# Layer 1 of a graph attention kernel: long tiles get their softmax in two or three groups of rows with all sums in PSUM

## The chip, the cores and the metric

The kernel runs on one core of a Trainium2 chip. The metric is the device time of one execution in microseconds; the time of the kernel before is 5602.67 us, the median of three runs (5597.33 to 5605.57). All arithmetic of the layers is in float32.

## The reference

A network of two graph attention layers on 10,000 nodes with 768 features, and 170,000 edges (80,000 random pairs in both directions and a loop at each node). The edges come sorted by their target `dst`. Every node gets a mean over the rows of its sources, weighted by a softmax over its own incoming edges; in layer 1 this is done for 4 heads of 256 columns, in layer 2 for one head of 768. `gat_conv` adds one more loop to each node.

```python
def gat_conv(x, edge_index, W, a_src, a_dst, bias, heads, out_ch, concat):
    ei = _add_self_loops(edge_index, n)
    src, dst = (ei[0], ei[1])
    xl = (x @ W).reshape(n, heads, out_ch)
    alpha_src = jnp.einsum('nhc,hc->nh', xl, a_src)
    alpha_dst = jnp.einsum('nhc,hc->nh', xl, a_dst)
    e = jax.nn.leaky_relu(alpha_src[src] + alpha_dst[dst], 0.2)
    m = jax.ops.segment_max(e, dst, num_segments=n)
    e = jnp.exp(e - m[dst])
    s = jax.ops.segment_sum(e, dst, num_segments=n)
    alpha = e / (s[dst] + 1e-16)
    msg = xl[src] * alpha[:, :, None]
    out = jax.ops.segment_sum(msg, dst, num_segments=n)
    ...

h0 = x
h = relu(layer_norm(gat_conv(x, ..., HEADS, HID, True), g1, be1))
h1 = h + (h0 @ Wr1 + br1)
h = layer_norm(gat_conv(h1, ..., 1, OUT_DIM, False), g2, be2) + (h1 @ Wr2 + br2)
result = layernorm(x + h)
```

## The kernel before

**Stages.** `prepare` sorts the nodes by their number of edges, while TensorE computes `table1`: a row for each node with 1024 columns of `x @ W1` and, behind them, 4 target terms, 4 source terms and a number, 1033 float32 in all. `ordered_layer1` then gathers and reduces these rows and writes `table2`, and `ordered_layer2` does the same for layer 2. A third path, `general_path`, is for inputs that don't fit and isn't run here.

**Tiles and slots.** A tile is 128 nodes, one on each partition. Since the nodes are sorted, all nodes of a tile have about as many edges; `SLOTS[t]` is the number of rows that tile t gathers for each of its nodes. A row or slot is therefore one gather of 128 rows of `table1`, at most 529 KB; empty places of a tile aren't loaded. There are 79 tiles and 1377 slots. `TURNS` puts the tiles in an order that grows from 8 slots (position 0) to 41 (position 39) and falls again to 9 (position 78). Positions 34 to 45 have 22, 22, 23, 24, 26, 41, 27, 25, 24, 23, 22, 22 slots; 33 and 46 have 21.

**The ring.** `Ring` holds `RING1` = 29 slots in SBUF. `ring.fetch(q + 1 + ring.size)` (L872) is called after row q has been added, and asks for the row that takes its place: a gather (L425) on POOL's queue, which waits there until the engines are done with the old row.

**One tile that fits into the ring** (`whole`, L779; 29 slots and less). `weights_of(t)` (L741) makes its softmax. `logits` (L473) adds the target's term to the source terms of all n rows (L479; two instructions where the ring wraps), applies the leaky slope (L189), takes the maximum over the rows (L483), subtracts it (L486), and lets ACT take the exponents (L487); then it turns the rows' numbers into slots for layer 2 (L490) and clears the last columns of the rows (L491). `normalised` (L494) doubles the loop's weight (L504), sums (L498), adds 1e-16 (L499), inverts (L500) and multiplies (L501). All of these are on DVE with 4 to 108 numbers a partition.

The rows are then added to `acc`, 128 x 1024 in PSUM, in three ways:

- the first 4 (`ON_PE1`) by PE: ACT writes 4 diagonal matrices a row with the weights (L730), and PE multiplies them with the row (L736);
- of the others, three in four (`shared`, L753) are multiplied in place by ACT (L510, four instructions a row) and added by DVE with one TENSOR_TENSOR (L517);
- one in four is weighted and added by DVE alone (L521, four SCALAR_TENSOR_TENSOR of 256 columns).

ACT multiplies `LEAD` = 3 rows ahead of DVE (L867).

**How tiles overlap.** The softmax of tile t+1 is begun inside the loop of tile t: its `logits` at row n-3, its `normalised` and the first two rows of PE's sums at row n-2 (L868), the other two at the head of the next turn (L796). This is done if `SLOTS[t + 1] + LEAD <= ring.size` (L864), which holds for all but positions 39 and 40. After the loop, the next turn takes the statistics of `acc` (L579, L581), normalises it (L593, L595), adds the product of x with `Wr1` (L807), transposes the outcome h on PE, multiplies it with `w2` (L829) and stores `table2`.

**The tile of 41 slots** doesn't fit into the ring. It isn't begun ahead, and goes through `attend_parts` (L524): three groups of rows with a running maximum. For each group there are `logits` with the old maximum (L485); 4 rows summed by PE into a PSUM tile of its own (`sums`), the others by DVE into `h`, 128 x 1024 in SBUF, which is cleared first (L531); ahead of each later group `sums` is added to `h` (L539) and `h` is multiplied by the exponent of old minus new maximum (`fade`, L541, L542, L545). At the end the sums are added and `divided` divides by the total (L436). Two thirds of the rows are multiplied by ACT, each just ahead of its addition.

**Queues and order.** Each engine executes its instructions in the order in which the code records them (`manual_schedule`); an instruction that waits holds back all behind it on its engine. Gathers of rows and of x stand in POOL's queue, the loads and stores of x, h and `table2` in SP's.

Of the kernel before, what the change touches and what calls it, by code (L numbers as in the profile page):

```python
# [28 lines left out]
F32 = mybir.dt.float32  # L29
# [6 lines left out]
P = 128  # L36
# [17 lines left out]
PARTED2 = 26  # L54

# [25 lines left out]
def gnn_kernel(ctx, tc, x, x_cols, src, dst, src_col, dst_col, W1, a_src1, a_dst1, b1, g1, be1, Wr1, br1,  # L81
# [421 lines left out]
    def doubled(e, t):  # L503
        nc.vector.tensor_scalar(e[:, 0], e[:, 0], loops[:, TURNS[t]:TURNS[t] + 1], None, op0=OP.mult)  # L504
# [7 lines left out]
    def weigh(acc, row, e, dh, first=None, shared=False):  # L512


        if shared:
            c = e.shape[1] * dh
            nc.vector.tensor_add(acc[:, :c], acc[:, :c], row[:, :c])  # L517
            return
        for h in range(e.shape[1]):
            s = slice(h * dh, (h + 1) * dh)  # L520
            nc.vector.scalar_tensor_tensor(acc[:, s], row[:, s], e[:, h:h + 1],  # L521
                                           (acc if first is None else first)[:, s], op0=OP.mult, op1=OP.add)

    def attend_parts(small, ring, acc, h_, ad, heads, dh, t, summed, between):  # L524


        c = heads * dh
        groups = -(-SLOTS[t] * 2 // ring.size)
        cuts = [FIRST[t] + SLOTS[t] * g // groups for g in range(groups + 1)]
        top = total = sums = None  # L530
        nc.vector.memset(acc[:, :c], 0.0)  # L531
        for lo, hi in zip(cuts, cuts[1:]):
            e, new = logits(small, ring, lo, hi, ad, heads, c, top)
            if lo == FIRST[t]:
                doubled(e, t)
            part = small.tile([P, heads], F32, name="part")
            nc.vector.reduce_sum(part, e.rearrange("p k h -> p h k"), axis=AX.X)
            if top is not None:
                nc.vector.tensor_add(acc[:, :c], acc[:, :c], sums[:, :c])  # L539
                fade = small.tile([P, heads], F32, name="fade")  # L540
                nc.vector.tensor_sub(fade, top, new)  # L541
                nc.scalar.activation(fade, fade, AF.Exp)  # L542
                for h in range(heads):
                    s = slice(h * dh, (h + 1) * dh)
                    nc.vector.tensor_scalar(acc[:, s], acc[:, s], fade[:, h:h + 1], None, op0=OP.mult)  # L545
                nc.vector.tensor_mul(fade, total, fade)
                nc.vector.tensor_add(part, part, fade)
            top, total = new, part
            m = min(ON_PE1, hi - lo - 1)
            pe = lo if hi == cuts[-1] else hi - m  # L550
            steps = summed(pe, e[:, pe - lo:], m)
            sums = next(steps)
            if pe == lo:
                for _ in steps:
                    pass
            alone = [q for q in range(lo, hi) if not pe <= q < pe + m]
            for k, q in enumerate(alone):
                shared = k >= len(alone) // 3
                if shared:
                    multiply(ring.slot(q), e[:, q - lo], dh)  # L560
                if k == len(alone) // 3 + 1:
                    for _ in steps:
                        pass
                weigh(acc, ring.slot(q), e[:, q - lo], dh, shared=shared)
                ring.fetch(q + 1 + ring.size)
            ring.fetch(hi + ring.size)
            between.pop(0)()
        nc.vector.tensor_add(acc[:, :c], acc[:, :c], sums[:, :c])
        divided(small, h_, acc, total, None, heads, dh)
# [116 lines left out]
    def ordered_layer1():  # L686
        nc.scalar.add_instruction(mybir.InstLoadActFuncSet(name=nc.get_next_instruction_name(), act_func_set_id=6, engine=nc.scalar.engine))
        with tc.tile_pool(name="b1", bufs=1) as pool, tc.tile_pool(name="small1", bufs=2) as small, \
# [32 lines left out]
            def on_pe(t):  # L721


                return min(max(SLOTS[t] // 2 - 5, 1), ON_PE1, SLOTS[t])
# [16 lines left out]
            def weights_of(t):  # L741

                n, m = SLOTS[t], on_pe(t)
                e, _ = logits(small, ring, FIRST[t], FIRST[t] + n, ring.slot(FIRST[t])[:, C1:C1 + H1], H1, C1)
                yield e
                normalised(small, e, H1, t)
                acc = ps_acc.tile([P, 2 * BANK], F32, name="acc")
                diagonals = pool.tile([P, ON_PE1 * H1, P], F32, name="diagonals")
                for lo, hi in ((0, min(m, 2)), (min(m, 2), m)):
                    summed(acc, diagonals, e, FIRST[t], lo, hi, m)  # L750
                    yield acc

# [22 lines left out]
            for t in range(NT + 1):  # L775
# [3 lines left out]
                whole = live and n <= ring.size  # L779
                if whole and not ready:  # L780
                    ahead = weights_of(t)
                    ready += itertools.islice(ahead, 2)

                def multiplied(upto):
                    nonlocal done
                    while whole and done < min(upto, n):
                        if shared(t, done):
                            multiply(ring.slot(FIRST[t] + done), e[:, done], DH1)
                        done += 1

                if whole:
                    e, acc = ready
# [3 lines left out]
                for _ in ahead:  # L796
                    pass
# [21 lines left out]
                if whole:  # L819
                    by_wr1()  # L820
# [26 lines left out]
                if live and not whole:  # L847
                    due(first + 1)
                    sums, acc = (ps_acc.tile([P, 2 * BANK], F32, name="acc") for _ in range(2))
                    ad = small.tile([P, H1], F32, name="ad")  # L850
                    nc.vector.tensor_copy(ad, ring.slot(FIRST[t])[:, C1:C1 + H1])

                    def some(q, e, m):
                        diagonals = pool.tile([P, ON_PE1 * H1, P], F32, name="diagonals")
                        for lo, hi in ((0, min(m, 2)), (min(m, 2), m)):
                            summed(sums, diagonals, e, q, lo, hi, m)
                            yield sums

                    h = pool.tile([P, C1], F32, name="h")
                    attend_parts(small, ring, h, acc, ad, H1, DH1, t, some,  # L860
                                 [by_wr1, lambda: due(n)] + [lambda: None] * n)
                ready = []
                ahead = iter(())
                if whole and t + 1 < NT and SLOTS[t + 1] + LEAD <= ring.size:  # L864
                    ahead = weights_of(t + 1)
                for k in range(n if whole else 0):
                    multiplied(k + 1 + LEAD)  # L867
                    if n - LEAD <= k < n - LEAD + 2:  # L868
                        ready += itertools.islice(ahead, 1)
                    if k >= first:  # L870
                        weigh(acc, ring.slot(FIRST[t] + k), e[:, k], DH1, shared=shared(t, k))
                    ring.fetch(FIRST[t] + k + 1 + ring.size)  # L872
                    due(k)
# [468 lines left out]
```

## Time and profile before

| | |
|---|---|
| runs, median (lowest, highest) | 5602.67 us (5597.33, 5605.57) |
| profiled execution | 5607.1 us, its span 5605.3 us |
| granted TensorE clock, mean | 0.93 |
| busy in the span: PE, DVE, ACT, POOL | 4888.6, 4294.8, 2813.9, 3242.1 us |
| layer 1, first to last write of h (L595) | 939.3 to 3410.7 us |

The span is what the profiler recorded from the first to the last instruction, and the time of the execution is a little longer. In the lists of waits a line names the waiting instruction, what released it, the microseconds in total, how often, and the longest.

DVE writes h once a tile (L595). The time from one of these writes to the next is the length of a tile; most of the softmax of the tile that follows lies in it too.

| position | slots | length, us | | position | slots | length, us |
|---|---|---|---|---|---|---|
| 20 | 17 | 29.5 | | 38 | 26 | 41.4 |
| 27 | 19 | 31.7 | | 39 | 41 | 81.0 |
| 30 | 20 | 33.5 | | 40 | 27 | 52.0 |
| 33 | 21 | 36.6 | | 41 | 25 | 43.9 |
| 34 | 22 | 39.3 | | 42 | 24 | 41.7 |
| 35 | 22 | 41.7 | | 43 | 23 | 41.5 |
| 36 | 23 | 43.1 | | 44 | 22 | 40.0 |
| 37 | 24 | 46.0 | | 45 | 22 | 39.1 |

### The profile page before, as it was taken

Reading aid. Unit: us, or ns where it says so; the run is one execution under the profiler, and the core shown is the slowest. Engines: PE = TensorE matmul, PEld = TensorE weight load, DVE = VectorE, ACT = ScalarE, POOL = GpSimd, SP = SyncE. Lnnn points to the kernel's source line nnn. Section 1 sums busy time; section 2 is a strip of 40 time slices with the busy share of each in tenths; the row PEclk is TensorE's granted clock in tenths of the full one; section 3 lists DMA queues with packets and bytes.
Section 4 is the critical chain, followed back from the end, with each engine's and each line's share of the span. In section 5 each row is a group of like instructions: output and inputs, shape, how many; then the busy total and the mean of one; then the engine's idle time right before and its main releaser. Section 6 shows DMA issues by size and latency. Waiting matters only on the chain. (4 is left out here: it accounts for less than half of the span.)

```text
span 5605.3 us, 59627 instructions
## 1 busy us (share of the span) xinstructions
PE 4888.6 (87%) x15188; PEld 2899.2 (52%) x15191; DVE 4294.8 (77%) x7761; ACT 2813.9 (50%) x8193; POOL 3242.1 (58%) x3159
## 2 busy tenths in 40 slices
PE   8999996999999875789999999899988888877765
PEld 3444443555555543455555555565655555555544
DVE  5783344999999887888999995888876866766676
ACT  3443344777788776777877773333322322222222
POOL 3447365556666556566666553666665666666664
PEclk9999998999999987899999999999998888888877
DMA  4333626999999987899999986999888888888885
GB/s 156 122 99 87 92 90 254 323 335 352 362 361 373 340 320 265 316 343 360 364 359 355 335 307 231 323 336 331 320 321 292 313 299 299 288 293 286 289 286 182
DMA packets 474307, 1591.37 MB, mean 284 GB/s; under 512 B 118328, under 2 KB 122488, under 8 KB 473959
## 3 DMA queue, kind: packets, MB, share of 16 engines
q0 software_dynamic: 322384, 1286.62, 64.8%
q1 hardware_dynamic: 149520, 297.43, 15.8%
q10 hardware_dynamic: 2054, 3.42, 0.2%
q8 instruction: 128, 2.10, 0.2%
q14 instruction: 221, 1.80, 0.1%
HBM read 1431.80 MB, written 177.29 MB: 287 GB/s over the span
## 5 line engine op out<-in xcount | busy, mean ns | idle before, releaser
L425 POOL DMA_INDIRECT ring<-table,slots x2675 | 2660.2, 994 | 1774.4 <-issue 542.1
L521 DVE SCALAR_TENSOR_TENSOR acc<-ring,e,acc 128x512 f32<-128x512 f32 (+1 forms) x2530 | 1578.3, 624 | 137.7 <-PE acc L736 46.1
L510 ACT ACTIVATE ring<-ring,e 128x256 f32<-128x256 f32 x3284 | 1338.3, 508 | 1.4 <-issue 1.2
L517 DVE TENSOR_TENSOR acc<-acc,ring 128x1024 f32<-128x1024 f32 x801 | 985.7, 1231 | 73.2 <-issue 1.9
L991 PE MATMUL big<-wr,w 128*128 128x512 f32 (+1 forms) x2464 | 876.7, 502 | 147.0 <-issue 145.5
L946 PE MATMUL big<-ring,diagonals 128*128 128x256 f32 x2754 | 746.9, 430 | 169.1 <-issue 138.7
L172 PE MATMUL big<-w,xT 128*128 128x512 f32 x1896 | 823.8, 596 | 26.5 <-DMA w<-in_W_dram 10.3
L172 PE MATMUL big<-wr,xT 128*128 128x512 f32 x1896 | 833.2, 596 | 0.2 <-issue 0.2
L829 PE MATMUL half<-w,hT 128*128 128x512 f32 (+1 forms) x2528 | 830.4, 486 | 0.0
L946 PEld LDWEIGHTS big<-ring,diagonals 128*128 128x128 f32 x2754 | 590.5, 218 | 331.3 <-issue 203.6
L991 PEld LDWEIGHTS big<-wr,w 128*128 128x128 f32 x2464 | 484.2, 197 | 504.0 <-issue 471.6
L945 ACT ACTIVATE diagonals<-ident,e 128x128 f32<-128x128 f32 x1377 | 423.9, 388 | 612.9 <-remote 230.0
L829 PEld LDWEIGHTS half<-w,hT 128*128 128x128 f32 x2528 | 477.8, 189 | 372.3 <-issue 332.7
L736 PE MATMUL acc<-ring,diagonals 128*128 128x256 f32 x1912 | 480.1, 408 | 204.8 <-ACT diagonals L730 179.6
L172 PEld LDWEIGHTS big<-w,xT 128*128 128x128 f32 x1896 | 361.3, 191 | 484.5 <-issue 466.3
L172 PEld LDWEIGHTS big<-wr,xT 128*128 128x128 f32 x1896 | 356.7, 192 | 420.3 <-issue 420.3
L736 PEld LDWEIGHTS acc<-ring,diagonals 128*128 128x128 f32 x1912 | 387.0, 205 | 290.7 <-ACT diagonals L730 200.8
L583 ACT ACTIVATE sd<-mv,eps 128x1 f32<-128x1 f32 x237 | 69.3, 292 | 697.5 <-DVE mv L581 451.6
L730 ACT ACTIVATE diagonals<-ident,e 128x128 f32<-128x128 f32 x956 | 293.0, 387 | 207.6 <-DVE e L501 165.4
L667 DVE TENSOR_TENSOR scr<-big,ad_b 128x1024 f32<-128x1024 f32 x79 | 96.7, 1224 | 377.5 <-ACT row L664 333.4
L672 POOL TENSOR_TENSOR row<-row,none 128x1024 f32<-128x1024 f32 x79 | 187.2, 2370 | 260.8 <-ACT row L664 258.4
L670 ACT ACTIVATE scr<-scr 128x256 f32<-128x256 f32 x632 | 253.6, 402 | 120.3 <-DVE scr L667 117.7
(185 smaller groups left out, 3430.6 us busy)
## 6 DMA issues: line engine op xcount, KB each, us to landing
ring<-table,slots POOLq DMA_INDIRECT x2675
table<-row SPq DMA_DIRECT2D x79, 516.0 KB
h_d<-hT SPq DMA_DIRECT2D x79, 512.0 KB
w<-h_d SPq DMA_DIRECT2D x77, 512.0 KB
table<-row SPq DMA_DIRECT2D x79, 385.0 KB
ring<-table SPq DMA_DIRECT2D x79, 385.0 KB
xT<-in_x_cols_dram SPq DMA_DIRECT2D x79, 384.0 KB
x_d<-xt SPq DMA_DIRECT2D x79, 384.0 KB
```

The lines of the kernel that those rows point to most:

```text
L172: nc.tensor.matmul(p[:, c:e], aT[:, j, :], w[:, j, c:e], start=(j == 0), stop=(j == k - 1))
L425: nc.gpsimd.indirect_dma_start(out=to, out_offset=None, in_=table, in_offset=bass.IndirectOffsetOnAxis(ap=index, axis=0), **more)
L510: nc.scalar.activation(row[:, s], row[:, s], AF.Copy, scale=e[:, h:h + 1])
L517: nc.vector.tensor_add(acc[:, :c], acc[:, :c], row[:, :c])
L521: nc.vector.scalar_tensor_tensor(acc[:, s], row[:, s], e[:, h:h + 1], (acc if first is None else first)[:, s], op0=OP.mult, op1=OP.add)
L670: nc.scalar.activation(m[:, s], m[:, s], AF.Copy, accum_out=row[:, C1 + i * H1 + h:C1 + i * H1 + h + 1])
L730: nc.scalar.activation(diagonals[:, k * H1 + i, :], ident, AF.Copy, scale=e[:, k, i:i + 1])
L736: nc.tensor.matmul(acc[:, c:d], diagonals[:, k * H1 + i, :], ring.slot(q + k)[:, c:d], start=(k == 0 and c % BANK == 0), stop=(k == m - 1 ...
L829: nc.tensor.matmul(q, hT[:, j, :], w2[:, j, c:c + q.shape[1]], start=(j == 0), stop=(j == K1 - 1))
L945: nc.scalar.activation(diagonals[:, (k - lo) % G, :], ident, AF.Copy, scale=e[:, k - lo, :])
L946: nc.tensor.matmul(to, diagonals[:, (k - lo) % G, :], ring.slot(at + k)[:, ON_PE2:C2], start=False, stop=(k == n - 1), skip_group_check=True)
L991: nc.tensor.matmul(r[:, c:d], hT[:, j, :], wr2[:, j, c:d], start=False, stop=(j == K1 - 1 and d < C2), skip_group_check=True)
```

## The change

Every tile now goes through the same loop, and `attend_parts` is gone. `cuts_of(t)` divides the rows of a tile: one group below `PARTED` = 22 slots, two from 22 to 29, three for 41. A cut that would fall on a row that DVE weights alone moves on by one, so that the first row of a later group is always one that ACT multiplies. The cuts are at 11 (22 and 23 slots), 13 (24 to 27 slots), and 13 and 27 (41 slots).

`weights_of(t)` makes the softmax of the first group alone, not yet divided by its sum, and begins PE's sums; this happens at the same places of the tile ahead as before, for every tile. The target's term is copied to `ad` first. For each later group it goes on inside the tile's own loop: eight rows ahead of the cut `logits` of the group with the old maximum, and the exponent `fade` of old minus new maximum; five rows ahead of the cut the new total, and in the last group the division of `fade` and of the group's weights by it. At the cut, `weigh` with `fade` multiplies all that is in `acc` and adds the row, in four SCALAR_TENSOR_TENSOR of 256 columns in place of one TENSOR_TENSOR. `acc` stays in PSUM throughout, also for the tile of 41 slots, of which only the first 4 rows are now summed by PE, and of the others three in four are multiplied by ACT. The condition on the ring's size at L864 is dropped.

Of the removed function only the ends are shown.

```diff
--- before.py
+++ after.py
@@ -52,6 +52,7 @@
 SHARE = 4
 ON_PE1 = 4
 PARTED2 = 26
+PARTED = 22
 
 
 def chunk_counts(n_edges):
@@ -509,9 +510,15 @@
             s = slice(h * dh, (h + 1) * dh)
             nc.scalar.activation(row[:, s], row[:, s], AF.Copy, scale=e[:, h:h + 1])
 
-    def weigh(acc, row, e, dh, first=None, shared=False):
-
-
+    def weigh(acc, row, e, dh, first=None, shared=False, fade=None):
+
+
+        if fade is not None:
+            for h in range(e.shape[1]):
+                s = slice(h * dh, (h + 1) * dh)
+                nc.vector.scalar_tensor_tensor(acc[:, s], acc[:, s], fade[:, h:h + 1], row[:, s],
+                                               op0=OP.mult, op1=OP.add)
+            return
         if shared:
             c = e.shape[1] * dh
             nc.vector.tensor_add(acc[:, :c], acc[:, :c], row[:, :c])
@@ -520,53 +527,6 @@
             s = slice(h * dh, (h + 1) * dh)
             nc.vector.scalar_tensor_tensor(acc[:, s], row[:, s], e[:, h:h + 1],
                                            (acc if first is None else first)[:, s], op0=OP.mult, op1=OP.add)
-
-    def attend_parts(small, ring, acc, h_, ad, heads, dh, t, summed, between):
...
-        divided(small, h_, acc, total, None, heads, dh)
 
     def pieces(a, width):
 
@@ -740,15 +700,50 @@
 
             def weights_of(t):
 
-                n, m = SLOTS[t], on_pe(t)
-                e, _ = logits(small, ring, FIRST[t], FIRST[t] + n, ring.slot(FIRST[t])[:, C1:C1 + H1], H1, C1)
-                yield e
-                normalised(small, e, H1, t)
+                n, m, at = SLOTS[t], on_pe(t), FIRST[t]
+                cuts = cuts_of(t)
+                ad = ring.slot(at)[:, C1:C1 + H1]
+                if len(cuts) > 2:
+                    own = ad
+                    ad = small.tile([P, H1], F32, name="ad")
+                    nc.vector.tensor_copy(ad, own)
+                e, top = logits(small, ring, at, at + cuts[1], ad, H1, C1)
+                yield {0: (e, None)}
+                if len(cuts) == 2:
+                    normalised(small, e, H1, t)
+                else:
+                    doubled(e, t)
+                    total = small.tile([P, H1], F32, name="total")
+                    nc.vector.reduce_sum(total, e.rearrange("p k h -> p h k"), axis=AX.X)
                 acc = ps_acc.tile([P, 2 * BANK], F32, name="acc")
                 diagonals = pool.tile([P, ON_PE1 * H1, P], F32, name="diagonals")
                 for lo, hi in ((0, min(m, 2)), (min(m, 2), m)):
-                    summed(acc, diagonals, e, FIRST[t], lo, hi, m)
+                    summed(acc, diagonals, e, at, lo, hi, m)
                     yield acc
+                for lo, hi in zip(cuts[1:], cuts[2:]):
+                    e, new = logits(small, ring, at + lo, at + hi, ad, H1, C1, top)
+                    fade = small.tile([P, H1], F32, name="fade")
+                    nc.vector.tensor_sub(fade, top, new)
+                    nc.scalar.activation(fade, fade, AF.Exp)
+                    yield
+                    part = small.tile([P, H1], F32, name="part")
+                    nc.vector.reduce_sum(part, e.rearrange("p k h -> p h k"), axis=AX.X)
+                    nc.vector.tensor_mul(total, total, fade)
+                    nc.vector.tensor_add(total, total, part)
+                    top = new
+                    if hi == n:
+                        nc.vector.tensor_scalar(total, total, 1e-16, None, op0=OP.add)
+                        nc.vector.reciprocal(total, total)
+                        nc.vector.tensor_mul(fade, fade, total)
+                        nc.vector.tensor_mul(e, e, total[:, None, :].to_broadcast([P, hi - lo, H1]))
+                    yield lo, (e, fade)
+
+            def cuts_of(t):
+
+                n = SLOTS[t]
+                groups = 1 if n < PARTED else -(-2 * n // ring.size)
+                cuts = [n * g // groups for g in range(groups + 1)]
+                return [c + (0 < c < n and not shared(t, c)) for c in cuts]
 
             def shared(t, k):
                 return (k - on_pe(t)) % SHARE > 0
@@ -776,25 +771,30 @@
                 live, events = t < NT, []
                 n = SLOTS[t] if live else 0
                 first = done = on_pe(t) if live else 0
-                whole = live and n <= ring.size
-                if whole and not ready:
+                cuts = cuts_of(t) if live else []
+                if live and not ready:
                     ahead = weights_of(t)
                     ready += itertools.islice(ahead, 2)
 
+                def row_of(k):
+                    lo = max(c for c in es if c <= k)
+                    return es[lo][0][:, k - lo], es[lo][1] if k == lo else None
+
                 def multiplied(upto):
                     nonlocal done
-                    while whole and done < min(upto, n):
+                    while done < min(upto, n):
                         if shared(t, done):
-                            multiply(ring.slot(FIRST[t] + done), e[:, done], DH1)
+                            multiply(ring.slot(FIRST[t] + done), row_of(done)[0], DH1)
                         done += 1
 
-                if whole:
-                    e, acc = ready
+                later = iter(())
+                if live:
+                    es, acc = ready
+                    es, later = dict(es), ahead
                 if last:
                     r_before, means = last
                     stats = deviation(small, pieces(means[:, :C1], BANK))
-                for _ in ahead:
-                    pass
+                next(later, None)
                 if full is not None:
                     store(t - 2)
                 moves = []
@@ -816,8 +816,7 @@
                     if live and t:
                         r = product(xT, wr1, C1, ps_r)
 
-                if whole:
-                    by_wr1()
+                by_wr1()
 
                 def to_layer2():
                     nonlocal full
@@ -844,31 +843,22 @@
                     while events and events[0][0] <= k:
                         events.pop(0)[1]()
 
-                if live and not whole:
-                    due(first + 1)
-                    sums, acc = (ps_acc.tile([P, 2 * BANK], F32, name="acc") for _ in range(2))
-                    ad = small.tile([P, H1], F32, name="ad")
-                    nc.vector.tensor_copy(ad, ring.slot(FIRST[t])[:, C1:C1 + H1])
-
-                    def some(q, e, m):
-                        diagonals = pool.tile([P, ON_PE1 * H1, P], F32, name="diagonals")
-                        for lo, hi in ((0, min(m, 2)), (min(m, 2), m)):
-                            summed(sums, diagonals, e, q, lo, hi, m)
-                            yield sums
-
-                    h = pool.tile([P, C1], F32, name="h")
-                    attend_parts(small, ring, h, acc, ad, H1, DH1, t, some,
-                                 [by_wr1, lambda: due(n)] + [lambda: None] * n)
                 ready = []
                 ahead = iter(())
-                if whole and t + 1 < NT and SLOTS[t + 1] + LEAD <= ring.size:
+                if live and t + 1 < NT:
                     ahead = weights_of(t + 1)
-                for k in range(n if whole else 0):
+                for k in range(n):
+                    if k + 2 * LEAD + 2 in cuts[1:-1]:
+                        next(later)
+                    if k + LEAD + 2 in cuts[1:-1]:
+                        lo, es_lo = next(later)
+                        es[lo] = es_lo
                     multiplied(k + 1 + LEAD)
                     if n - LEAD <= k < n - LEAD + 2:
                         ready += itertools.islice(ahead, 1)
                     if k >= first:
-                        weigh(acc, ring.slot(FIRST[t] + k), e[:, k], DH1, shared=shared(t, k))
+                        weights, fade = row_of(k)
+                        weigh(acc, ring.slot(FIRST[t] + k), weights, DH1, shared=shared(t, k), fade=fade)
                     ring.fetch(FIRST[t] + k + 1 + ring.size)
                     due(k)
                 due(DEGREES)
```

More of the change, by code (lines that the diff above doesn't have):

```diff
@@ L522, in weigh @@
                                            (acc if first is None else first)[:, s], op0=OP.mult, op1=OP.add)
-    def attend_parts(small, ring, acc, h_, ad, heads, dh, t, summed, between):
[L527 to L554, printed above, removed]
-                    pass
[L556 to L568, printed above, removed]
-        divided(small, h_, acc, total, None, heads, dh)
     def pieces(a, width):
@@ L795, in ordered_layer1 @@
                     stats = deviation(small, pieces(means[:, :C1], BANK))
-                for _ in ahead:
-                    pass
+                next(later, None)
                 if full is not None:
```

## The prediction

> **What bounds the kernel now.** I read the slices first, because the changed tiles sit in one place. Layer 1 runs from slice 6 (840 us) to slice 24 (3500 us); its long tiles are in slices 13 to 17, where the DMA row falls to 6 and the granted clock to 7.
>
> ```profile
> DVE  5783344999999887888999995888876866766676
> PEclk9999998999999987899999999999998888888877
> DMA  4333626999999987899999986999888888888885
> ```
>
> The busy times of two stretches say what is lost there. 1872 to 2460 holds the tiles at positions 33 to 45 (bounds: the L595 write of h, once a tile), 1640 to 1766 the tiles of 19 and 20 rows before them.
>
> ```profile
> 1872.00:2460.00 588.00, 428.44 (x1387) 267.45 (x1386) 483.25 (x772) 419.96 (x1124) 343.87 (x335) 0.85 0.86 310
> 1640.00:1766.00 126.00, 117.49 (x401) 70.23 (x400) 114.92 (x185) 101.92 (x275) 82.05 (x81) 1.00 0.99 370
> ```
>
> The columns after the stretch and its length are PE, PEld, DVE, ACT and POOL busy, granted clock, DMA share and GB/s. The 19-row tiles run at 370 GB/s with DVE busy 91%. The long tiles get 310 GB/s and DVE is busy 82%. At 370 GB/s their 182 MB (588 x 310) would take 493 us: transfers aren't the floor there, something makes them start late. The waits of DVE name it, first in the long tiles, then (last line) in 1640 to 1766:
>
> ```profile
> DVE e L479 <- DMA ring<-table,slots: 35.6, 12, 5.9
> DVE acc L521 <- PE acc L736: 19.1, 12, 4.7
> DVE h L517 <- ACT ring L510: 6.0, 13, 1.7
> DVE e L479 <- issue: 4.6, 2, 3.1
> DVE h L531 <- PE half L708: 2.3, 1, 2.3
> ...
> DVE acc L521 <- PE acc L736: 1.9, 4, 0.6
> ```
>
> L479 is the first instruction of a softmax; it reads every row of the next tile, and DVE stands (40.2 us with the "issue" line) until the last of them lands. Tile 35 (22 rows) shows it:
>
> ```profile
> 1964.46 2.06 DVE L521 SCALAR_TENSOR_TENSOR acc<-ring,e,acc 128x256 f32<-128x256 f32 x4
> 1966.63 3.91 DVE L517 TENSOR_TENSOR acc<-acc,ring 128x1024 f32<-128x1024 f32 x3
> 1970.58 2.06 DVE L521 SCALAR_TENSOR_TENSOR acc<-ring,e,acc 128x256 f32<-128x256 f32 x4
> 1972.74 2.57 DVE L517 TENSOR_TENSOR acc<-acc,ring 128x1024 f32<-128x1024 f32 x2
> 1975.89 0.24 DVE L479 TENSOR_TENSOR e<-ring 128x80 f32<-128x80 f32 x1 [0.57 <-DMA ring<-table,slots]
> 1979.59 0.17 DVE L479 TENSOR_TENSOR e<-ring 128x12 f32<-128x12 f32 x1 [3.46 <-DMA ring<-table,slots]
> ...
> 1991.18 1.22 DVE L807 SCALAR_TENSOR_TENSOR h<-h,big 128x1024 f32<-128x1024 f32 x1
> ```
>
> Four L521 are a row that DVE weights itself, one L517 a row that ACT has multiplied. The next tile has 23 rows and the ring 29, so its last row is asked for when row 22+23-30 = 15 is done: the last of the three L517 from 1966.63, at 1970.54. L479 is released at 1979.59. One turn-around is 9.05 us.
>
> To separate work from waiting I added up, for every DVE instruction of a tile, the time to the next start where no wait lies between (L517 into acc 1.335 us, that is 1.231 and a gap of 0.104; L521 into acc 0.525, that is 0.489 and 0.035). For the tiles of 13 to 17 rows this gives the measured length to 0.3 us in nearly all, so DVE's own work bounds those. For positions 33 to 45 it gives 513 us of the measured 587.4: 74 us are waits, of which those above account for 67.6.
>
> **What the change takes away.** A tile is asked for its first 11 to 13 rows when its softmax begins three rows before the end of the tile ahead; their slots were freed near row 22+11-30 = 3 of that tile. That wait goes, except for the 2.4 us at the end of position 45, whose successor has 21 rows and stays whole: 37.8 us. Position 39 (41 rows) now starts ahead, multiplies three rows ahead and isn't begun with a memset: its L517 (6.0), L531 (2.3) waits go, and the late sums of position 40 (4.7 of the 19.1). Where the sums are on time the same wait is 0.6 (the last line of that fence). Six tiles (22 or 23 rows) put their second softmax, about 2 us of work, just ahead of it; there it is covered, and 7 tiles keep 0.6: of 19.1, 14.9 go. Some 10 us of small waits are left over or unnamed in the 74; I let 3 go. Sum: 37.8 + 6.0 + 2.3 + 14.9 + 3 = 64 us.
>
> **What it adds on DVE**, which becomes the bound of these tiles (all other engines have room: ACT 420, POOL 344 of 588). Per tile cut in two, each duration with 0.035 of gap: the copy of ad 0.20; second logits on 11 to 14 rows, add 0.25 to 0.36, leaky 0.25, maximum 0.29, maximum with the old one 0.20, subtract 0.25, slot numbers and memset 0.2 (they overlap their neighbours), together 1.45; fade, part, and three products or sums of 4 numbers 1.06 (L541 to L547 show 0.154 to 0.232 each). The first logits are shorter by 0.23. The row at the cut becomes four instructions in place of one L517: 4 x 0.525 - 1.335 = 0.77. Sum 3.25 us, for 11 tiles 35.8.
>
> Position 39 is costed alone. These four groups (columns: count, busy, mean ns) set it:
>
> ```profile
> L517 DVE TENSOR_TENSOR acc<-acc,ring 128x1024 f32<-128x1024 f32 x170 | 209.3, 1231 | 16.4 <-remote 0.5 <-DVE acc L521 0.5
> L521 DVE SCALAR_TENSOR_TENSOR acc<-ring,e,acc 128x256 f32<-128x256 f32 x252 | 123.3, 489 | 27.3 <-PE acc L736 19.1
> L517 DVE TENSOR_TENSOR h<-h,ring 128x1024 f32<-128x1024 f32 x20 | 24.5, 1226 | 7.2 <-ACT ring L510 6.0 <-ACT diagonals L730 0.5 <-DVE h L517 0.2
> L521 DVE SCALAR_TENSOR_TENSOR h<-ring,e,h 128x256 f32<-128x256 f32 x36 | 14.5, 476 | 0.0
> ```
>
> Rows it weights itself: 36 instructions into h, in SBUF, took 14.5 us, 0.403 each; now 40 into acc, in PSUM, at 0.525, 21.0: +6.5. Multiplied rows: 20 took 25.7 with gaps, now 25 at 1.335, 33.4: +7.7. Fading: 8 of 0.31 (L545: 2.5 busy), now 8 of 0.525: +1.7. Away go three additions of sums (3.7), a memset (0.9), four divisions (2.0) and two small ones (0.4): -7.0. Net +8.9. Only 4 of its rows go to PE in place of 12; ACT gets 28 more multiplications of about 0.40 from start to start and loses 32 diagonals of 0.30, and stays under DVE.
>
> [...] The trace has 13 ns in duration but 122 ns from start to start (0.525 against 0.403), as instructions into h overlap. [...]
>
> **Sum.** 587.4 - 64 + 35.8 + 8.9 = 568; 19 us less. The profiled execution's span is 5605.3 (5607.1 with what lies around it), 4.4 above the median of 5602.7, a part in a thousand; layer 2 and the rest of layer 1 keep their time. 5602.7 - 19 is 5583.
>
> **What no row shows.** The fading instruction reads acc, a pointer and the row. Nearest rows: L545 (one tensor, 372 ns) and L521 on 512 columns (752 ns). 52 of them: -6 to +14 us round the 489 ns I take, since it has the operands and size of that row. The new wait of the second softmax: none at best; at worst all 40.2 us come back. I take none: it is issued eight rows ahead of the cut, and its last row is asked for 12 to 18 us before. In the timeline above, from row 15's end at 1970.54 to the end of the wide h instructions at 1992.4 lie 22 us, 18 without the 4 us of wait, against the 9.05 needed. The tightest are positions 39 and 40: after row 23 of 26, or 38 of 41, come two rows (2.7 to 3.4), the sum of the first part (0.5), statistics (1.6), three wide instructions (4.2), row 4 (2.1) and 0.6 of wait on PE, 12 us. ACT's exponents cost 0.45 us a cut and are asked for three rows ahead; if that cover failed, 0.5 x 13 = 6 us. On POOL one gather of x moves ahead of 20 gathers in position 39; it is 0.97 us of that queue. The order on SP is as it was, and so is what is loaded.
>
> [...] The row has 9.05 from the freed slot, with POOL's turn and other transfers in it. [...]
>
> **Rivals.**
> Only the row waits go. The waits on PE, on ACT and the small ones (36.6 us with position 45's) stay, because the diagonals still queue behind ACT's multiplications: 557.7 (work, 513 + 44.7) + 36.6 = 594, 7 us more: 5609, no difference that can be told. For it: the PE wait is in all 12 tiles. Against: in tiles of 20 rows it is 0.6.
> The second softmax takes the wait over. Place: ahead of row 3 or 5 of each tile (at the cut less eight), in DVE's queue, with L521 and L517 of that tile behind it and ACT's exponents, so multiplied rows, behind those. Price: the saved 37.8 us return while the 44.7 of work stay: 5583 + 38 = 5621, slower. It decides from a turn-around of 12 us (positions 39, 40) and fully from about 20. Against: 9.05 measured, with DMA busier than it will be (182 MB in 568 us is 321 GB/s).
> Transfers pace it. If a tile can't move more than the 333 GB/s seen at position 42 (24 rows), 182 MB take 547 us, under the 568: hidden. It would need 310 GB/s to be the bound: no change, 5603.
>
> **How the numbers follow.** Forecast 0.64, only the row waits 0.18, second softmax 0.12, transfers 0.06. Two runs of this kernel differ by up to 0.15%, so under 0.2% (11 us) counts as no change. The forecast's own range is 5570 (remaining waits and cheap fading, 13 us off) to 5598 (dear fading); it gives 0.57 faster and 0.07 same. The second case gives 0.15 same, 0.03 slower, the fourth 0.03 faster and 0.03 same; the third 0.01 same, 0.11 slower. Faster 0.60, same 0.26, slower 0.14. The range takes in transfers as the bound and half of the second softmax's wait (19 us): 5570 to 5604.
>
> **What would show it.** L479 waits on the DMA in positions 33 to 44 gone, fade instructions of 0.49 us, position 39 near 72 us in place of 81 and position 40 near 47 in place of 52, while those of 22 rows gain at most 3 and 38 gets longer by 3 to 4: I expect the gain in few tiles. L479 waiting early in a tile would make me wrong, and so would DVE waiting for ACT at the rows behind a cut.

## The result, and the profile after

The changed kernel takes 5576.89 us, the median of 7 runs (5567.96 to 5587.24); the kernel before, run beside it, 5602.67 (7 runs, 5597.33 to 5607.92). The ratio is 0.996, with a 95% interval of 0.9948 to 0.9972: some 22 us faster, clear of the noise. 5583 had been forecast. The profiled execution took 5571.7 us, its span is 5569.9.

The stretch of the changed tiles, positions 33 to 45 from one write of h to another (its line is L555 in the new file), runs from 1871.2 to 2433.8: 562.6 us in place of 587.4. The tiles ahead of it take 928.2 (932.8 before), those behind it 949.1 (951.2), layer 2 2187.1 (2194.6), differences that say little: other profiles of the same code have 928 to 934 us ahead of the stretch (but for one chip, told below) and 949 to 952 behind it, and layer 2 took 2194 in a second profile of the changed kernel. This is the row of that stretch in the busy times (PE, PEld, DVE, ACT, POOL, granted clock, DMA share, GB/s):

```profile
1871.00:2434.00 563.00, 412.22 (x1327) 253.62 (x1326) 511.04 (x951) 422.20 (x1141) 338.37 (x335) 0.85 0.91 324
```

DVE is busy 511 of 563 us (91%) where it was busy 483 of 588 (82%), with 951 instructions in place of 772: more work in less time. Where the time came from stands in its waits there:

```profile
DVE acc L528 <- PE acc L696: 7.2, 7, 1.7
DVE acc L524 <- issue: 0.5, 1, 0.5
DVE h L553 <- PE acc L696: 0.5, 1, 0.5
DVE acc L519 <- DVE acc L519: 0.5, 1, 0.5
DVE e L480 <- DMA ring<-table,slots: 0.2, 1, 0.2
```

The last line is the wait for rows, 0.2 us in place of 40.2 (L480 is the old L479). That 0.2 us is at a first softmax, the one of position 38 at the end of position 37; no second softmax waited. What was paid for it are these groups (count, busy us, mean ns, idle before):

```profile
L524 DVE TENSOR_TENSOR acc<-acc,ring 128x1024 f32<-128x1024 f32 x184 | 226.4, 1230 | 15.6 <-issue 0.5
L528 DVE SCALAR_TENSOR_TENSOR acc<-ring,e,acc 128x256 f32<-128x256 f32 x291 | 142.3, 489 | 17.0 <-PE acc L696 7.6
L519 DVE SCALAR_TENSOR_TENSOR acc<-acc,fade,ring 128x256 f32<-128x256 f32 x52 | 25.6, 492 | 5.8 <-DVE acc L519 0.5
```

An instruction of the fading row, which no line of before showed, takes 492 ns; 489 had been assumed. But 5.8 us of idle stand before the 52 of them, and the four of a row last 2.28 us below, so they are 0.596 us apart from start to start where 0.525 had been assumed. A second softmax, in the tile of 41 rows, in DVE's order of time:

```profile
2114.98 2.06 DVE L528 SCALAR_TENSOR_TENSOR acc<-ring,e,acc 128x256 f32<-128x256 f32 x4 [0.57 <-PE acc L696]
2116.96 0.21 DVE L480 TENSOR_TENSOR e<-ring,ad 128x56 f32<-128x56 f32 x1
...
2118.41 3.89 DVE L524 TENSOR_TENSOR acc<-acc,ring 128x1024 f32<-128x1024 f32 x3
2122.22 0.25 DVE L730 TENSOR_REDUCE part<-e 128x4 f32<-128x56 f32 x1
...
2122.65 2.05 DVE L528 SCALAR_TENSOR_TENSOR acc<-ring,e,acc 128x256 f32<-128x256 f32 x4
2124.81 3.91 DVE L524 TENSOR_TENSOR acc<-acc,ring 128x1024 f32<-128x1024 f32 x3
...
2130.92 2.28 DVE L519 SCALAR_TENSOR_TENSOR acc<-acc,fade,ring 128x256 f32<-128x256 f32 x4
```

The softmax follows on the row before it without a gap, the sum of the weights finds ACT's exponents done, and the fading row at the cut comes in its turn. By position:

| position | slots | before, us | after, us |
|---|---|---|---|
| 33 | 21 | 36.6 | 34.9 |
| 34 to 37 | 22, 22, 23, 24 | 170.1 | 159.2 |
| 38 | 26 | 41.4 | 46.5 |
| 39 | 41 | 81.0 | 70.9 |
| 40 | 27 | 52.0 | 47.0 |
| 41, 42 | 25, 24 | 85.6 | 86.7 |
| 43 to 45 | 23, 22, 22 | 120.6 | 117.4 |

### The profile page after: what moved, and what is told of

It is laid out like the page before. It is cut to its first block, busy times and chain, and to the rows that moved or that the text cites. A ratio compares the mean times of both kernels' runs of the same rounds, so it can differ in the third digit from the quotient of the medians.

```text
span 5569.9 us, 59759 instructions
## 1 busy us (share of the span) xinstructions
PE 4871.4 (87%) x15124; PEld 2881.6 (52%) x15127; DVE 4321.6 (78%) x7940; ACT 2816.4 (51%) x8211; POOL 3234.8 (58%) x3159
## 5 line engine op out<-in xcount | busy, mean ns | idle before, releaser
L528 DVE SCALAR_TENSOR_TENSOR acc<-ring,e,acc 128x256 f32<-128x256 f32 (+1 forms) x2570 | 1597.7, 622 | 135.0 <-PE acc L696 31.5
L524 DVE TENSOR_TENSOR acc<-acc,ring 128x1024 f32<-128x1024 f32 x815 | 1002.6, 1230 | 69.1 <-issue 0.9
L696 PE MATMUL acc<-ring,diagonals 128*128 128x256 f32 x1848 | 464.1, 408 | 215.0 <-ACT diagonals L690 211.2
L696 PEld LDWEIGHTS acc<-ring,diagonals 128*128 128x128 f32 x1848 | 373.9, 205 | 297.8 <-ACT diagonals L690 234.9
```

The lines of the kernel that those rows point to most:

```text
L696: nc.tensor.matmul(acc[:, c:d], diagonals[:, k * H1 + i, :], ring.slot(q + k)[:, c:d], start=(k == 0 and c % BANK == 0), stop=(k == m - 1 ...
```

## The experiments

Ratios are to the kernel before on the same chip. Four runs (only the two longest tiles cut, not begun ahead, more work on DVE, a row less for DVE) were on a chip whose layer 2 takes 1850 us in place of 2190 (told at the end), so their times are near 5250. Tiles that run the same code take the same time there in and behind the stretch (with positions 39 and 40 not begun ahead, 41 to 45 took 204.2 us, as in the change; 46 to 78 took 950 to 952 in all four), and these stretches are compared across chips. Positions 1 to 32 are not alike: 938 to 942 us there, 928 to 934 elsewhere at 29 rows.

**The change once more.**

> The change itself, as it is, for a comparison on one chip with the runs beside it: 0.996 of before; positions 33 to 45 at 562 to 566 us.

It took 5573.86 us against 5602.52, ratio 0.9945 (0.9931 to 0.9958); positions 33 to 45 took 563.4 us. The stretch repeats within 1 us. The two ratios, 0.996 and 0.9945, have overlapping intervals; layer 2 alone took 2187 us in one profile of this kernel and 2194 in the other.

**Only the two longest tiles cut.**

```diff
-PARTED = 22
+PARTED = 27
...
-                if live and t + 1 < NT:
+                if live and t + 1 < NT and cuts_of(t + 1)[1] + LEAD <= ring.size:
```

> Only the tiles of 27 and 41 rows (positions 40 and 39) are cut; 22 to 26 rows stay whole. Theory (DVE bounds the cut tiles, the wait for rows bounds the whole ones): position 39 stays at 71 us, 40 near 48 (41's 25 rows are awaited again, 2 us), 38 at 43 to 44 (no cut of its own, but 39's first softmax), 33 to 37 and 41 to 45 as before (206.7 and 206.2 us), so 162 against 174.4 us at 38 to 40: 12 us faster than before, 5591. Rival (the long tile alone pays, the shorter ones pay their added DVE work for nothing): as fast as the change or faster, 5577 or less.

It took 5248.67 against 5259.13, ratio 0.9981 (0.9972 to 0.999), 10 us, and positions 33 to 45 took 579.0 us. So the tiles of 22 to 26 rows are worth the other 16 us of the stretch, and the rival falls. Positions 38 to 40 took 43.4, 71.8 and 51.8: 167.0, not 162; at the last DVE stood 3.1 us for the 25 whole rows of the tile that follows, and its own list holds 26.4 us for rows and 18.9 for PE's sums.

**Positions 39 and 40 not begun ahead.**

```diff
-                if live and t + 1 < NT:
+                if live and t + 1 < NT and SLOTS[t + 1] + LEAD <= ring.size:
```

> The change, but positions 39 and 40 (41 and 27 rows) aren't begun in the tile ahead. Theory: the first softmax and PE's sums of these two then lie open at the head of their turn, DVE waits 4 to 5 us for PE's sums in each (4.7 was seen at position 40 before): positions 38 to 40 get 8 to 12 us longer than the 164.4 of the change, 5587. Rival (the start ahead is worth nothing, since DVE has the same work wherever it stands): within 2 us of the change.

It took 5240.55, ratio 0.9966 (0.9952 to 0.9979). Positions 38 to 40 took 172.3 us, 7.9 more than in the change, and DVE waited 3.8 and 4.1 us for PE's sums at 39 and 40, where the change has 0.6 each. This is the lower edge of what was expected. The start ahead is worth about 8 of the 24.7 us, by the wait that had been named.

**More work on DVE.**

```diff
+                    more = small.tile([P, ring.size, H1], F32, name="more")
+                    for _ in range(12):
+                        nc.vector.tensor_add(more[:, :hi - lo], e, e)
                     yield lo, (e, fade)
```

> The change with 12 more additions of 44 to 56 numbers on DVE at each cut, into a tile that nobody reads. 12 x about 0.24 us is 2.9 us a cut, 13 cuts, 37 us of DVE. Theory (DVE bounds the cut tiles): positions 34 to 45 get 33 to 38 us longer, slower than before, near 5613. Rival (transfers or the landing of rows pace these tiles): less than 12 us of it is seen.

It took 5273.11, ratio 1.0029 (1.0019 to 1.004), slower than before, and positions 34 to 45 took 566.8 us in place of 527.8, 39.0 more. The largest group of the additions:

```profile
L741 DVE TENSOR_TENSOR more<-e 128x44 f32<-128x44 f32 x72 | 14.7, 204 | 2.5
```

At 0.204 us and 0.035 of gap, 12 of them are 2.9 us a cut; all 156 are busy for 32.6 us, with 5.3 of gaps before them. These 38 us of added work are all seen in the time: DVE bounds the cut tiles, and nothing paces them from behind.

**A ring of 28 rows, in the kernel before and in the changed one.**

```diff
-RING1 = 29
+RING1 = 28
```

> The kernel before with a ring of 28 rows in place of 29: each row is asked for one row later, about 1.5 us of DVE. Theory (the softmax of a whole tile waits for the landing of its last row, 9 us after it is asked for): the wait at the first instruction of the softmax grows from 40 to 50 to 58 us in positions 33 to 45, and 26 rows no longer start ahead, 4 to 5 us: 600 to 608 us in place of 587; tiles of 19 to 21 rows outside lose about 1 us each, 8 to 12 us. Slower by 0.4 to 0.5%. Rival (transfers as a whole pace the tiles): no change in positions 33 to 45.

> The change with a ring of 28 rows. Theory: the second softmax has 12 to 18 us from the asking to the use, 1.5 less is still above 9, so positions 34 to 45 stay within 3 us of the change's 528; the whole tiles of 19 to 21 rows lose 8 to 12 us as in the kernel before. Rival (the second softmax is just in time): 10 us or more are lost in positions 34 to 45, waiting at the second softmax.

The kernel before took 5627.84, ratio 1.0046 (1.0031 to 1.0062), and positions 33 to 45 601.4 us in place of 587.4. The changed one took 5593.93, ratio 0.9984 (0.9974 to 0.9994), and the stretch 563.2 in place of 562.6. The waits of DVE in it, first before, then changed:

```profile
DVE e L479 <- DMA ring<-table,slots: 47.7, 13, 7.7
DVE acc L521 <- PE acc L736: 21.8, 12, 4.6
```

```profile
DVE acc L528 <- PE acc L696: 7.7, 7, 2.2
DVE e L480 <- DMA ring<-table,slots: 0.9, 3, 0.5
```

One row less in the ring costs whole tiles and leaves cut tiles as they were. Outside the stretch, where all tiles are whole, the changed kernel lost 7.0 us ahead and 12.5 behind it, more than the 8 to 12 expected.

**Smaller rings**, in the change, with the cuts kept (24 rows likewise).

```diff
-RING1 = 29
+RING1 = 26
...
-                groups = 1 if n < PARTED else -(-2 * n // ring.size)
+                groups = 1 if n < PARTED else -(-2 * n // 29)
```

> The change with a ring of 26 rows and the same cuts. Every row is asked for three rows, about 4.4 us, later than with 29. Estimated margins between asking and the second softmax: 13 to 14 us at 22 to 25 rows, 11 at 26, 7 to 8 at 27 and 41 rows. Theory (a row needs about 9 us): waits of 1 to 2 us at the second softmax of positions 39 and 40, none elsewhere; positions 34 to 45 at 529 to 533 (528 with 29). Rival (the second softmax is just in time everywhere): over 30 us more. The whole tiles of 18 to 21 rows wait longer, outside these positions.

> The same with 24 rows: five rows, about 7.4 us, later. Margins 10 to 11 us at 22 to 25 rows, 7 to 8 at 26, 4 to 5 at 27 and 41 rows, where the third softmax of the latter has 4 too. Theory: waits of 1 to 2 us at position 38, 4 to 5 at 40, 8 to 10 in two places at 39; positions 34 to 45 at 541 to 547, the waits on L480 behind the first rows of a tile. Rival 1 (just in time everywhere): over 50 us more. Rival 2 (rows land in 4 us or less): within 3 us of 528.

Single executions took 5622.69 and 5716.19 us (the kernel before 5572.8 on that chip). Positions 34 to 45 took 533.4 and 542.7 us, the first at the edge of its range and the second in it, but not for the reasons given. With 26 rows no second softmax waits; 3.3 us are the wait at position 45 for its whole successor, which the expectation had put outside. With 24 rows the same wait is 6.2 us, and the second softmax waits at 39 and at 40, once in each, 5.9 and 2.4 us; waits at 38 and at a second place in 39 had been expected too and didn't come:

```profile
2204.92 0.22 DVE L480 TENSOR_TENSOR e<-ring,ad 128x56 f32<-128x56 f32 x1 [5.89 <-DMA ring<-table,slots]
...
2228.48 0.28 DVE L480 TENSOR_TENSOR e<-ring,ad 128x28 f32<-128x28 f32 x2
```

This is position 39 with 24 rows. Its second softmax waits 5.89 us for a row whose gather began on POOL at 2196.23, 8.7 us earlier; the third begins 2.3 us after the gather of its last row (2226.17) and waits for nothing. The wait that the rival foresaw exists, then, but not with three rows less in the ring, only with five. Why the third doesn't wait shows in what the DMA moved, in two slices of 2 us (the last number is GB/s):

```profile
2202.00:2204.00 2.00, 2.00 (x6) 0.94 (x5) 0.00 (x0) 0.00 (x0) 0.00 (x0) 1.00 0.63 243
2226.00:2228.00 2.00, 0.00 (x0) 0.00 (x0) 1.89 (x2) 0.00 (x0) 1.48 (x2) 0.50 0.03 0
```

Empty places of a tile aren't loaded, and the gathers of the longest tile's last rows move next to nothing. Its third softmax was never a tight place.

**A row less for DVE.** PE sums 5 rows of a cut tile, 3 of them begun in the tile ahead.

```diff
-                return min(max(SLOTS[t] // 2 - 5, 1), ON_PE1, SLOTS[t])
+                return ON_PE_PARTED if SLOTS[t] >= PARTED else min(max(SLOTS[t] // 2 - 5, 1), ON_PE1, SLOTS[t])
...
-                        nc.scalar.activation(diagonals[:, k * H1 + i, :], ident, AF.Copy,
+                        nc.scalar.activation(diagonals[:, k % ON_PE1 * H1 + i, :], ident, AF.Copy,
...
-                for lo, hi in ((0, min(m, 2)), (min(m, 2), m)):
+                for lo, hi in ((0, max(min(m, 2), m - 2)), (max(min(m, 2), m - 2), m)):
```

> The change, and in the cut tiles PE sums 5 rows in place of 4 (3 of them begun in the tile ahead). DVE loses one row a tile: 10 x 1.335 and 2 x 2.1 us, 17.5 in all. Theory (DVE bounds): positions 34 to 45 get 12 to 17 us shorter (528 less that), 5562; less if PE's sums come late, up to 1.6 us a tile. Rival (transfers pace them, 36 us at 22 rows): under 5 us.

It took 5240.21, ratio 0.9966 (0.9954 to 0.9978), and positions 33 to 45 567.3 us, 4.7 longer than in the change. DVE's busy time in the stretch fell from 511 to 497 us, but its waits took it back:

```profile
DVE acc L529 <- PE acc L697: 21.2, 12, 3.5
DVE part L731 <- ACT e L489: 5.9, 6, 1.0
```

The theory had named late sums, up to 1.6 us a tile, as what could shrink the gain, but not that they would take all of it: PE's sums cost 14 us more than in the change, 1.2 a tile, and the exponents 6. Waits for rows come to 0.7 us, so transfers didn't hold it.

**The same, with all of PE's sums begun in the tile ahead** (all five rows recorded at row n-2) and the new total four rows ahead of the cut. The code is shown against the version before it.

```diff
-                for lo, hi in ((0, max(min(m, 2), m - 2)), (max(min(m, 2), m - 2), m)):
+                for lo, hi in ((0, min(m, 2)), (min(m, 2), min(m, 4)), (min(m, 4), m)):
                     summed(acc, diagonals, e, at, lo, hi, m)
-                    yield acc
+                    if len(cuts) == 2 and (lo, hi) != (m, m):
+                        yield acc
+                if len(cuts) > 2:
+                    yield acc
+                    yield acc
...
-                    if k + LEAD + 2 in cuts[1:-1]:
+                    if k + LEAD + 1 in cuts[1:-1]:
```

> As with 5 rows on PE, but all of PE's sums of a cut tile are begun in the tile ahead, and the new total is taken four rows ahead of the cut, not five. Theory (with 5 rows DVE lost 17 us of work and stood 14 us longer for PE's sums and 6 us for ACT's exponents): both waits go, positions 33 to 45 come to 545 to 550 us in place of 562.7, 13 to 17 us faster than the change. Rival (something else, transfers above all, holds the tiles at 562): within 5 us of the change.

It took 5574.99, ratio 0.9951 (0.9939 to 0.9963), where the change itself had 0.9945 beside it: no difference in the whole. Positions 33 to 45 took 556.0 us, 7 less, half of what was expected. The waits on the exponents were gone; those on PE's sums were still 14.0 us, and 3.2 were for ACT at the write of h, where ACT has the diagonals to make first. The reason shows in the changed kernel itself, in 2 us slices around the sums for position 40 (PE's records in brackets behind its busy time, two for each matmul; granted clock as the third from the right):

```profile
2176.00:2178.00 2.00, 1.43 (x3) 1.17 (x4) 1.93 (x4) 1.89 (x7) 0.99 (x1) 0.50 0.83 312
...
2180.00:2182.00 2.00, 2.00 (x8) 1.66 (x8) 1.86 (x4) 0.76 (x4) 1.70 (x2) 0.77 0.87 267
2182.00:2184.00 2.00, 2.00 (x11) 1.72 (x11) 1.85 (x2) 2.00 (x9) 1.15 (x2) 1.00 0.86 264
```

PE had stood for 38.75 us. Its first records come at a clock of 0.50, 0.43 us apart, and only 4.4 us after the first one at 1.00 and 0.22 apart. Sums that start here as soon as the weights are there start at half speed, so a row more on PE is late.

**The sums two rows earlier**, in the change, and in the version with 5 rows on PE.

```diff
+                sooner = 2 if live and t + 1 < NT and len(cuts_of(t + 1)) > 2 else 0
...
-                    if n - LEAD <= k < n - LEAD + 2:
+                    if n - LEAD - sooner <= k < n - LEAD - sooner + 2:
```

> The change, with the first softmax of a cut tile and PE's first sums two rows earlier in the tile ahead. In the traces so far PE begins these sums from rest and puts its first 10 to 14 matmuls 0.43 us apart, the later ones 0.21, so that the 16 of them end 3.1 to 4.3 us after DVE begins the write of h, DVE being ready for them at 2.6. Theory: begun 2.8 us sooner, the first half runs while DVE still adds rows, and most of the 7.2 us of wait for PE's sums goes: positions 33 to 45 at 556 to 559 in place of 562.7. Rival (what PE does between the two halves makes it start from rest again): as the change.

> As with 5 rows on PE, all begun in the tile ahead, and now the first softmax and PE's sums two rows earlier. Theory (its 14 us of wait for PE's sums, and 3 on ACT behind the diagonals, stood because PE starts these 20 matmuls from rest at half the rate): begun 2.8 us sooner, both shrink to 2 to 5 us, positions 33 to 45 at 542 to 547 in place of 556.0, which would be 16 to 20 us faster than the change. Rival (transfers hold the tiles): 553 to 556, with waits of DVE on rows.

The change with earlier sums took 5557.09 against 5577.44, ratio 0.9956 (0.9939 to 0.9972), and its stretch 562.4 us: nothing gained in the stretch, as the rival had it. Its second burst of PE's sums for position 40 (the first is 16 records from 2176.84 to 2183.00), and slices round it:

```profile
2184.88 5.41 PE L696 MATMUL acc<-ring,diagonals 128*128 128x256 f32 x16 [1.89 <-ACT diagonals L690]
```

```profile
2182.00:2184.00 2.00, 1.00 (x5) 0.54 (x3) 1.90 (x4) 0.00 (x0) 1.12 (x3) 1.00 0.62 174
...
2186.00:2188.00 2.00, 2.00 (x6) 1.60 (x5) 1.89 (x2) 2.00 (x7) 0.25 (x1) 0.50 0.96 322
```

PE ends the first two rows early at full clock, rests until the other two come at the head of the next turn, and the clock is at 0.50 again from 2186 to 2188. The rest between the two bursts was 1.89 us. With 5 rows on PE, all begun ahead and two rows earlier, PE doesn't stop between them, and runs the 40 records for position 40 in one piece, at a clock of 0.50 and 0.64 in the slices from 2161 and 2163 and of 1.00 in all four from 2165 to 2173:

```profile
2161.03 10.59 PE L697 MATMUL acc<-ring,diagonals 128*128 128x256 f32 x40 [34.53 <-ACT diagonals L691]
```

It took 5536.27 against 5577.44, ratio 0.9924 (0.9905 to 0.9944), and the stretch takes 542.4 us, 20 less than the change. The longest waits of DVE from 1872 to 2420:

```profile
DVE acc L529 <- PE half L669: 2.7, 3, 1.9
DVE acc L529 <- PE acc L697: 1.9, 2, 1.3
```

This version beats the kernel before, and on the same chip it is 21 us ahead of the change with earlier sums, whose stretch is as long as the change's. DVE is busy 494 of 542 us of the stretch, again 91%.

## Why the prediction was right

**What bounds the tiles.** That whole tiles wait for the landing of their last row, and that DVE's own work bounds the cut ones, was shown from both sides: a row less in the ring cost the kernel before 14 us in the stretch and the changed one 0.6, and 38 us of added DVE work cost 39 us. The 9.05 us from freed slot to release were read from one tile; read in the same way from the trace of before, eleven tiles of the stretch take 5.0 to 9.9. The margins of 12 to 18 us are above all of these. One reading was off without a consequence: in slices 13 to 17 the DMA row falls to 7, not to 6.

**The waits taken away.** 64 of the 74 us were to go, leaving 10.4. Left are 8.9 us of named waits: 0.2 for rows, 7.7 for PE's sums and 1.0 others. Two terms were off and nearly cancel, which is luck. PE's sums kept 7.7 in place of 4.2: the six tiles of 22 and 23 rows show no such wait, as named, but the seven others keep 1.0 us each in place of 0.6. And the 2.4 us for the whole successor of position 45 didn't come back: its softmax began 7.4 us after the last slot had been freed and found the row there, where before it had come after 9.9. Why the row came sooner isn't shown.

**The work added.** This term was too large. 44.7 us were forecast, 557.7 in all. 562.6 less the named waits is 553.7, so 41 were added if the 513 stand. Counted alike in both kernels, by the named waits alone (70.5 us before), it is 37. Small instructions cost less than their durations with a gap of 0.035: with the second softmax, L528 and L524 of the tile of 41 rows start 3.43 us apart (2114.98, 2118.41), without it 2.16 (2122.65, 2124.81), so that it costs 1.27 us where 1.45 had been taken. The fading row cost more: 4 x 0.596 in place of 4 x 0.525, 0.28 us a cut or 3.7 in all. Of the two prices without a row, then, the fading instruction's duration was right and its distance wrong, and the wait of the second softmax is none, as taken. The measured 24.8 us of the stretch against 19 forecast are 4 us of work and 1.5 of small waits that I had left in, if the 513 stand.

**Sums in PSUM.** Position 39 gained 10.1 us (9 forecast), although its sums cost DVE more in PSUM than they had in SBUF: before, an instruction that weights 256 columns of a row took 489 ns into acc and 476 into h, and 0.525 and 0.403 us from start to start. The waits it shed (7.9 us for rows of position 40, 6.0 on ACT, 2.3 on PE) paid for that. Position 40 came out at the 47 us named, 38 got 5.1 us longer where 3 to 4 were named.

**Where the gain lies.** This point was wrong: I expected it in few tiles. The long ones, 38 to 40, gave 10.0 us net and 33 to 37 gave 12.6, of which position 37's 3.4, 36's 3.2 and 35's 3.2 are the largest. With only 27 and 41 rows cut, the stretch was 16 us longer than in the change. Behind the long tile (41 to 45) the waits for rows and PE had been 17 us, and added work in five tiles took most of that back: the cut paid 2.1 us there, and at 25 and 24 rows it cost 1.1.

**The rivals.** "Only the row waits go" falls: the waits on PE went from 19.1 to 7.7 us, and those on ACT (6.0) and ahead of the memset (2.3) are gone; without the start ahead of two tiles, 7 us for PE come back. "The second softmax takes the wait over" falls for 29 rows, but it is a real limit: with 24 rows 5.9 and 2.4 us of it came at the two positions that had been named as the tightest. "Transfers pace it" falls with the version that took the stretch to 542.4 us, at 336 GB/s.

## What to carry to other kernels

A softmax over a whole tile in a ring buffer needs all rows at once, and so leaves only what the ring has beyond the tile for the time from asking to landing; cut in groups with a running maximum, it needs half of them, and here the same ring then had three rows to spare. Add up the engine's own time from start to start before you count such a gain: of the 65 us of waits removed, the added instructions took back some 41. And look at what the bounding engine waits for next: a row moved to PE first lost 5 us in the stretch, and paid 20 once PE started its sums early enough to be past its slow start (in the change 4.4 us at a clock of 0.50), without a rest between their halves.

## What the runs showed of the hardware

Layer 2, which no run changed, took 1850 us on one chip and 2155 to 2200 on the others, with the same program. From 3500 to 5000 us, first on that chip (the version with only the longest tiles cut), then in the profile of before:

```profile
3500.00:5000.00 1500.00, 1408.10 (x4935) 957.35 (x4934) 1343.52 (x2706) 501.34 (x1581) 1129.92 (x1167) 0.96 0.98 367
```

```profile
3500.00:5000.00 1500.00, 1301.89 (x4225) 851.97 (x4225) 1151.48 (x2333) 436.01 (x1343) 947.69 (x981) 0.91 0.89 311
```

Granted clock 0.96 against 0.91, and 367 GB/s against 311. Whether one of the two slows the other wasn't tried. On one of the others layer 2 took 2183 to 2200 us in four profiles, a spread as large as most of the effects studied here, so that stretches of layer 1 told kernels apart that whole times could not.
